# Moving the splits of the second half's weights over slots 54 to 61 in an attention and FFN kernel

## The chip, the cores and the metric

The kernel runs on one core of one Trainium2 chip. The metric is the device time of one launch in microseconds (us); the kernel before took 2179.8 us, the median of three runs (2177.97 to 2180.97). TensorE (PE) does the matrix products, VectorE (DVE), ScalarE (ACT) and GpSimd (POOL) the element-wise work, and SyncE (SP) issues nearly all DMAs (transfers) from one queue, in order.

## The reference

x is 4096 tokens by 512. One layer of linear attention, a layer norm, an FFN with Hadamard transforms, and a second layer norm:

```python
q, k, v = x @ Wq.T, x @ Wk.T, x @ Wv.T      # 16 query heads, 4 key/value heads of 128
q, k = rope(q), rope(k)
qf, kf = elu(q) + 1, elu(k) + 1
# running over the tokens: state += k v^T, z += k; out = (q state) / (q z + eps)
x = layernorm(x + out @ Wo.T)
x = layernorm(x + ffn(x))
```

The change lies in the attention part alone.

## The kernel before

**Precision by splitting.** All products are of float32 accuracy, made of the rounded type float32r: an operand is split into a high half and a low half, and a product is three matmuls (high by high, high by low, low by high). `hilo` does a split: ScalarE copies the raw tile into the high half (line 94), and VectorE or GpSimd subtracts the high half from the raw one to make the low half (line 95).

**Two halves.** The attention runs twice over the tokens: the first half with query heads 0 to 7 and key/value heads 0 and 1, the second with the others. Each half has 16 blocks of 256 tokens. A half's weights are twelve tiles of 128 x 512: eight of q, two of k, two of v. Their high and low halves, 24 tiles, stay in the pool `wres` (28 tiles) for the whole half.

**Slots.** A loop runs over 128 slots, four for each block: slot i works at block n = i // 4, key/value head g and pair of chunks p. In slot i, in the order of the program, the kernel does the query projection of slot i + 5 (`proj_q`, 24 matmuls, line 339), and by the slot's place in its block the key projection of block n + 1 (`proj_k`, first slot, also line 339), the value projection of block n + 1 (`proj_v`, second slot, line 287, tile `ps_v`), the transposes of k (third slot, line 376, `pt`) or the state (line 391, `ps_s`). `ps_v`, `pt` and `ps_s` share one PSUM buffer, so `ps_v` can start when VectorE has read the last `ps_s` (line 402). Then come the scores of slot i + 1 (lines 434 and 435), the product with v and the state, `av` (lines 468 and 469), and last the finishing of the scores of slot i + 1: VectorE lines 444 and 445, GpSimd two `affine_select` (line 448). ScalarE copies `av`'s result out at line 472, its last step in a slot but for a small copy (line 477) in every second one. Rotary work: ScalarE lines 319 and 320, GpSimd line 321, VectorE 322, 325, 329, ScalarE 326 and 420, VectorE 422.

**The change of weights.** The second half starts at slot 64, so its projections are due from slot 59 on: heads q(0,0) and q(0,1) in slot 59, q(0,2), q(0,3) and both tiles of k in slot 60, q(1,0), q(1,1) and both of v in slot 61, q(1,2) and q(1,3) in slot 62. `turn(i)`, called at the end of slot i, reads raw weights (`fetch`) and splits them (`splits`); V or G says which engine makes the low half. Raw tiles are put into `praw` (three buffers, free again when the low half has been made) or into free tiles of `wres`.

**What sets the order.** The Tile framework's planner orders each engine's instructions by modelled times: one that is traced later may be put ahead of one that is not ready. `pin` (and `dma(..., True)`) keeps an instruction behind the one traced just before it on its engine. So a pinned low half on GpSimd in `turn(i)` stands behind the last `affine_select` of slot i + 1's scores, one on VectorE behind line 445 of these, a high half behind ScalarE's last copy of slot i, and a raw read on SP's queue behind the DMAs of slot i. In a slot at the second place of its block the last of these are the four `vd` writes of `proj_v`.

```python
i = S.activation(hi, src, AF.Copy)                              # line 94
j = eng.tensor_tensor(lo, src, hi.bitcast(F32), ALU.subtract)   # line 95
```

Of the kernel before, what the change touches and what calls it, by code (L numbers as in the profile page):

```python
# [43 lines left out]
def kernel(  # L44
# [6 lines left out]
    V, S, G, T = nc.vector, nc.scalar, nc.gpsimd, nc.tensor  # L51

    def dma(dst, src, pin=False):
        if dst.dtype == F32R:
            dst = dst.bitcast(F32)
        if src.dtype == F32R:
            src = src.bitcast(F32)
        i = nc.sync.dma_start(dst, src)  # L58
        if pin:
            tc.keep_in_program_order(i)  # L60

    cpool = ctx.enter_context(tc.tile_pool(name="cpool", bufs=1))
    wres = ctx.enter_context(tc.tile_pool(name="wres", bufs=28))
    praw = ctx.enter_context(tc.tile_pool(name="praw", bufs=3))
# [28 lines left out]
    def hilo(hi, lo, src, eng=V, pinned=False):  # L93
        i = S.activation(hi, src, AF.Copy)  # L94
        j = eng.tensor_tensor(lo, src, hi.bitcast(F32), ALU.subtract)  # L95
        if pinned:
            pin(i)
            pin(j)
# [87 lines left out]
    with ExitStack() as es:  # L186
# [39 lines left out]
        def turn(i):  # L226
            q = lambda g, h: (("q", 1, g, h), wq[8 + 4 * g + h])
            k = lambda g: (("k", 1, g), wk[2 + g])
            v = lambda j: (("v", 1, j), wv[1, :, j * 512:(j + 1) * 512])
            splits = {55: [(q(0, 0), V), (q(0, 1), G)], 56: [(q(0, 2), V)], 57: [(q(0, 3), G), (k(0), V)],  # L230
                      58: [(k(1), V), (q(1, 0), G)], 59: [(q(1, 1), G), (v(0), V), (v(1), V)],
                      60: [(q(1, 2), G), (q(1, 3), V)]}
            fetch = {53: [q(0, 0), q(0, 1), q(0, 2)], 55: [k(0), k(1), q(0, 3)],
                     56: [q(1, 0), q(1, 1), v(0), v(1), q(1, 2), q(1, 3)]}
            for (key, _), eng in splits.get(i, ()):
                hi, lo = (wres.tile([128, 512], F32R, tag="w", name=n) for n in ("wh", "wl"))
                hilo(hi, lo, RAW0.pop(key), eng, True)
                W[key] = hi, lo
            for m, (key, src) in enumerate(fetch.get(i, ())):
                pool, tag = (praw, "raw") if i == 53 or m < (2 if i == 55 else 1) else (wres, "w")  # L240
                RAW0[key] = pool.tile([128, 512], F32, tag=tag, name="raw")
                dma(RAW0[key], src, True)

# [347 lines left out]
        for i, (n, g, p) in enumerate(slots):  # L591
# [61 lines left out]
            for x in gsc:  # L653
                go(x)
            gq = gq2
            turn(i)
            if i == 107:
                o_load(0, None, None)
# [407 lines left out]
    with ExitStack() as es:  # L1066
# [23 lines left out]
        for n in range(NS):  # L1090
# [15 lines left out]
            for s, tag in enumerate(SEQ):  # L1106
# [3 lines left out]
                for u in (1, 0):  # L1110
# [3 lines left out]
                    i = 0  # L1114
# [11 lines left out]
                    if s in (1, 4, 6):  # L1126
                        src, k, q = {1: (ps, 0, 0), 4: (bank.get(("b", u)), 4, 3), 6: (ps, 2, 1)}[s]
# [68 lines left out]
    with ExitStack() as es:  # L1196
# [54 lines left out]
        for idx, (n, s) in enumerate(order):  # L1251
# [25 lines left out]
            tag = SEQ[s]  # L1277
# [14 lines left out]
            i = 0  # L1292
# [98 lines left out]
```

## Time and profile before

| what | value |
|---|---|
| median of the runs | 2179.8 us |
| profiled execution: own time; span | 2179.87 us; 2178.2 us |
| busy, share of the span: PE, DVE, ACT, POOL | 98%, 79%, 63%, 61% |
| granted TensorE clock | 0.997 |
| attention loop on PE (line 339, first and last start) | 8.9 to 827.2 us |
| one block in the second half (four slots) | 25.44 us |

Where the slots lie in time is read from ScalarE's copy at line 472, one for each slot:

| slot | 53 | 54 | 55 | 56 | 57 | 58 | 59 | 60 | 61 | 62 |
|---|---|---|---|---|---|---|---|---|---|---|
| starts at, us | 386.36 | 390.74 | 396.85 | 406.95 | 414.10 | 418.79 | 425.62 | 434.05 | 443.02 | 449.70 |

Times in timelines are counted from the start of the span. "Busy" of PE overstates its work, since one matmul's record of some 0.28 us covers the issue of the next ones, which start every 0.113 us; so the number of matmuls in a stretch is read beside the busy time. What stands in brackets at the end of a line of the timeline is the engine's idle time ahead of the instruction, and what ended it.

### The profile page before, as it was taken

The numbers are of one execution on the slowest core, as the hardware profiler recorded it, in microseconds if no ns is written. First come the engines' busy times: TensorE is split into PE (matmuls) and PEld (weight loads), VectorE is DVE, ScalarE is ACT, GpSimd is POOL, SyncE is SP. The second block draws the span as 40 slices with busy tenths as digits, with TensorE's granted clock in tenths as the row PEclk, the third lists the DMA queues.
The fourth block names the chain that finished last, engine by engine and source line by source line (L and its number), as shares of the span: only waits on it lengthen the run. The fifth ranks groups of instructions, "written<-read, shape, count | busy, mean of one in ns | idle before, by whom it ended". The sixth has DMA issues, their size and how long they took to land.

```text
span 2178.2 us, 42193 instructions
## 1 busy us (share of the span) xinstructions
PE 2140.6 (98%) x14319; PEld 1947.6 (89%) x14319; DVE 1728.9 (79%) x2675; ACT 1378.9 (63%) x2490; POOL 1321.8 (61%) x1104
## 2 busy tenths in 40 slices
PE   8999999999999998999999999999999999999998
PEld 8999999999999997887788788888888888999998
DVE  8999999899999997888998766776866766675655
ACT  8877877777777775443444476655655655565554
POOL 5777767666666666487888256565655555543332
PEclk9999999999999999999999999999999999999999
DMA  6666666656666666989988886876766767897784
GB/s 225 214 221 212 225 220 200 211 183 196 190 201 202 208 187 226 348 245 292 281 289 265 272 277 219 248 243 196 248 207 193 249 191 211 263 307 256 234 261 140
DMA packets 360553, 503.88 MB, mean 231 GB/s; under 512 B 68012, under 2 KB 187052, under 8 KB 356498
## 3 DMA queue, kind: packets, MB, share of 16 engines
q1 hardware_dynamic: 360338, 501.19, 72.1%
q8 instruction: 113, 1.85, 0.4%
q14 instruction: 102, 0.84, 0.1%
HBM read 282.76 MB, written 156.76 MB: 202 GB/s over the span
## 4 chain that ended last, share of the span: by engine, by line
PE 68%; DVE 12%; DMA 7%; issue 4%; POOL 4%; ACT 3%; SPq 2%; DVEq 0%; POOLq 0%; ACTq 0%
PE ps_a L1117 14%; PE ps_qk L339 12%; PE ps_da L1298 8%; PE ps_b L1117 7%; PE ps_wo L180 7%; PE ps_num L468 4%; PE ps_db L1298 4%; PE ps_c L1117 4%; PE ps_v L287 2%; DMA rb<-rec_d 2%; PE ps_dc L1298 2%; SPq L58 2%; DVE ps_qk L322 1%; PE ps_s L391 1%; DMA yraw<-yq_d 1%
## 5 line engine op out<-in xcount | busy, mean ns | idle before, releaser
L339 PE MATMUL ps_qk<-xh,wh 128*128 128x256 f32 x1280 | 354.9, 277 | 1.6 <-DVE x L325 0.9
L339 PE MATMUL ps_qk<-xh,wl 128*128 128x256 f32 x1280 | 354.0, 277 | 0.0
L339 PE MATMUL ps_qk<-xl,wh 128*128 128x256 f32 x1280 | 353.7, 276 | 0.0
L1099 POOL TENSOR_TENSOR cc<-cc 128x512 f32<-128x512 f32 x96 | 146.1, 1525 | 270.4 <-ACT cc L1096 129.5
L95 DVE TENSOR_TENSOR wol<-A,woh 128x512 fp32r<-128x512 f32 x217 | 226.4, 1050 | 94.7 <-ACT woh L94 84.0
L448 POOL TENSOR_SCALAR_AFFINE_SELECT A<-A 64x512 fp32r<-64x512 f32 x256 | 202.7, 792 | 131.1 <-DVE am L444 91.2
L321 POOL TENSOR_TENSOR sw<-sw,csb 128x512 f32<-128x512 f32 x160 | 213.9, 1337 | 76.2 <-ACT sw L320 64.8
L339 PEld LDWEIGHTS ps_qk<-xh,wh 128*128 128x128 f32 x1280 | 240.5, 188 | 4.7 <-DVE ql L422 1.5
L339 PEld LDWEIGHTS ps_qk<-xh,wl 128*128 128x128 f32 x1280 | 240.5, 188 | 1.5 <-DVE wl L95 0.2
L339 PEld LDWEIGHTS ps_qk<-xl,wh 128*128 128x128 f32 x1280 | 240.4, 188 | 1.0
L94 ACT ACTIVATE woh<-A 128x512 fp32r<-128x512 f32 x217 | 135.0, 628 | 122.5 <-PE ps_b L1117 72.8
L1117 PE MATMUL ps_a<-yoh,woh 128*128 128x512 f32 x512 | 199.9, 391 | 3.1 <-ACT sv L1124 2.6
L95 POOL TENSOR_TENSOR hal<-hraw,hah 128x512 fp32r<-128x512 f32 x74 | 98.1, 1327 | 172.7 <-PE ps_da L1298 59.6
L1117 PE MATMUL ps_a<-yol,woh 128*128 128x512 f32 x512 | 199.4, 389 | 0.0
L94 ACT ACTIVATE hah<-hraw 128x512 fp32r<-128x512 f32 x212 | 132.1, 631 | 106.3 <-PE ps_da L1298 54.2
L1117 PE MATMUL ps_a<-yoh,wol 128*128 128x512 f32 x512 | 196.7, 390 | 0.0
L95 DVE TENSOR_TENSOR hal<-hraw,hah 128x512 fp32r<-128x512 f32 x138 | 99.2, 727 | 90.1 <-PE ps_da L1298 39.0
L1124 ACT ACTIVATE sv<-ps_a,wsc 128x512 f32<-128x512 f32 x192 | 126.8, 679 | 34.7 <-PE ps_a L1117 34.4
L180 PE MATMUL ps_wo<-wh,oh 128*128 128x512 f32 x368 | 144.4, 393 | 0.0
L180 PE MATMUL ps_wo<-wh,ol 128*128 128x512 f32 x368 | 144.0, 391 | 0.0
L180 PE MATMUL ps_wo<-wl,oh 128*128 128x512 f32 x368 | 143.5, 390 | 0.0
L868 POOL TENSOR_TENSOR o<-nt,rb 128x512 f32<-128x512 f32 x62 | 86.8, 1400 | 74.0 <-DVE ol L95 44.1
(306 smaller groups left out, 7274.4 us busy)
## 6 DMA issues: line engine op xcount, KB each, us to landing
hraw<-hop_d SPq DMA_DIRECT2D x224, 256.0 KB
num_d<-num SPq DMA_DIRECT2D x128, 256.0 KB
rb<-rec_d SPq DMA_DIRECT2D x128, 256.0 KB
hop_d<-hS SPq DMA_DIRECT2D x128, 256.0 KB
vd<-vhl SPq DMA_DIRECT2D x128, 252.0 KB
nt<-num_d SPq DMA_DIRECT2D x30, 1024.0 KB
A<-in_wug_dram SPq DMA_DIRECT2D x93, 256.0 KB
hop_d<-cc SPq DMA_DIRECT2D x64, 256.0 KB
```

The source lines that it names most:

```text
L94: i = S.activation(hi, src, AF.Copy)
L95: j = eng.tensor_tensor(lo, src, hi.bitcast(F32), ALU.subtract)
L180: T.matmul(ps, l[:, h], r, start=i == 0, stop=i == 47)
L321: G.tensor_tensor(sw, sw, sinb, ALU.mult)
L339: T.matmul(ps[:, j], W[key][wa][:, k * 128:(k + 1) * 128], B[xa][:, k], start=i == 0, stop=i == 11)
L448: G.affine_select(ah, ah.bitcast(F32), pattern=[[0, 8], [1, 64]], compare_op=ALU.is_ge, fill=0.0, base=0, channel_multiplier=-1)
L468: T.matmul(ps[:, c2], l, r, start=i == 0, stop=i == len(ops) - 1)
L868: i = G.tensor_tensor(o32, c["nt"][:, 4 * g:4 * g + 4], rb, ALU.mult)
L1099: G.tensor_tensor(x, x, c.pop(("g", q)), ALU.mult)
L1117: T.matmul(ps, w[:, u, k], y[:, k], start=first and i == 0, stop=i == 5, skip_group_check=not first)
L1124: S.activation(x, ps, AF.Copy, scale=sc)
L1298: T.matmul(pj[j], ops[qd][al][:, r, js], BW[s][bl][ip], start=first and (i == 0 or i == 3 and pj is ps), stop=i >= 45 or last and i == 23, ...
```

## The change

Which slot splits which tile, and on which engine the low half is made; one `turn` per slot:

| slot | before: splits | after: splits | before: reads | after: reads |
|---|---|---|---|---|
| 52 | | | | q00, q01, q02 |
| 53 | | | q00, q01, q02 | |
| 54 | | q00 V | | q03 |
| 55 | q00 V, q01 G | q01 G | k0, k1, q03 | k0 |
| 56 | q02 V | q02 V, q03 G | q10, q11, v0, v1, q12, q13 | k1, v0, v1 |
| 57 | q03 G, k0 V | k0 V | | q10 |
| 58 | k1 V, q10 G | k1 V, v0 G | | q11, q12 |
| 59 | q11 G, v0 V, v1 V | q10 V, v1 G | | q13 |
| 60 | q12 G, q13 V | q11 G | | |
| 61 | | q12 G, q13 V | | |

VectorE makes six low halves in place of seven, GpSimd six in place of five. The number of reads and of high halves stays at twelve each. One raw tile (v1) is put into `wres` in place of six.

```diff
-            splits = {55: [(q(0, 0), V), (q(0, 1), G)], 56: [(q(0, 2), V)], 57: [(q(0, 3), G), (k(0), V)],
-                      58: [(k(1), V), (q(1, 0), G)], 59: [(q(1, 1), G), (v(0), V), (v(1), V)],
-                      60: [(q(1, 2), G), (q(1, 3), V)]}
-            fetch = {53: [q(0, 0), q(0, 1), q(0, 2)], 55: [k(0), k(1), q(0, 3)],
-                     56: [q(1, 0), q(1, 1), v(0), v(1), q(1, 2), q(1, 3)]}
+            splits = {54: [(q(0, 0), V)], 55: [(q(0, 1), G)], 56: [(q(0, 2), V), (q(0, 3), G)], 57: [(k(0), V)],
+                      58: [(k(1), V), (v(0), G)], 59: [(q(1, 0), V), (v(1), G)], 60: [(q(1, 1), G)],
+                      61: [(q(1, 2), G), (q(1, 3), V)]}
+            fetch = {52: [q(0, 0), q(0, 1), q(0, 2)], 54: [q(0, 3)], 55: [k(0)], 56: [k(1), v(0), v(1)],
+                     57: [q(1, 0)], 58: [q(1, 1), q(1, 2)], 59: [q(1, 3)]}
...
-                pool, tag = (praw, "raw") if i == 53 or m < (2 if i == 55 else 1) else (wres, "w")
+                pool, tag = (wres, "w") if (i, m) == (56, 2) else (praw, "raw")
```

## The prediction

> **What bounds the kernel now.** I first read the page: PE is busy 98% of the span, at a granted clock of 0.997, so only time in which PE stands still can be won. Then I cut the attention into stretches of one block (25.44 us). These are the lines of four of them; the columns are the stretch, its length, each engine's busy time with its number of instructions, the granted clock, and DMA's share and rate.
>
> ```profile
> 378.70:404.20 25.50, 25.40 (x222) 24.92 (x221) 21.43 (x35) 19.27 (x36) 13.33 (x15) 1.00 0.56 169
> 404.20:429.60 25.40, 23.96 (x199) 22.85 (x199) 23.90 (x41) 21.75 (x42) 18.69 (x18) 1.00 0.79 252
> 429.60:455.00 25.40, 22.35 (x184) 21.18 (x184) 24.58 (x38) 18.41 (x35) 15.62 (x16) 1.00 0.34 109
> 480.50:505.90 25.40, 25.40 (x226) 25.17 (x226) 23.93 (x39) 20.07 (x38) 16.98 (x17) 1.00 0.61 194
> ```
>
> The two middle stretches, where the weights change, hold 199 and 184 matmuls against 226 in a full one: 27 and 42 missing, at 0.113 us each 3.1 + 4.7 = 7.8 us. That is all that this change can win where it stands. The fourth line shows PE full again afterwards, so a loss or gain here reaches the end of the attention whole.
>
> Next I asked who waited for whom between 390 and 455 us (sum, times, longest).
>
> ```profile
> PE ps_v L287 <- DVE s L402: 3.4, 2, 2.5
> ...
> ACT wh L94 <- DMA raw<-in_wq_dram: 3.0, 1, 3.0
> ...
> DVE wl L95 <- ACT wh L94: 2.6, 1, 2.6
> ```
>
> PE waits for VectorE (the buffer that `ps_v` takes over), ScalarE once for a raw weight, VectorE for ScalarE behind it. The timelines of ACT, SP, PE, DVE and POOL place these waits.
>
> ```profile
> 400.68 0.64 ACT L94 ACTIVATE wh<-raw 128x512 fp32r<-128x512 f32 x1 [2.99 <-DMA raw<-in_wq_dram]
> ...
> 390.27 3.88 SPq L58 DMA_DIRECT2D vd<-vhl  x4
> 394.21 2.57 SPq L58 DMA_DIRECT2D raw<-in_wq_dram  x3
> ...
> 418.90 4.20 SPq L58 DMA_DIRECT2D vd<-vhl  x4
> 423.20 0.72 SPq L58 DMA_DIRECT2D xh<-xs_d  x1
> ...
> 406.44 0.38 PE L287 MATMUL ps_v<-wh,xh 128*128 128x256 f32 x1 [0.89 <-DVE s L402]
> 436.71 0.35 PE L287 MATMUL ps_v<-wh,xh 128*128 128x256 f32 x1 [2.48 <-DVE s L402]
> ...
> 431.56 2.38 DVE L95 TENSOR_TENSOR wl<-raw,wh 128x512 fp32r<-128x512 f32 x2
> 436.16 0.41 DVE L402 TENSOR_TENSOR s<-ps_s,s 128x256 f32<-128x256 f32 x1
> ...
> 431.05 1.74 POOL L321 TENSOR_TENSOR sw<-sw,csb 128x512 f32<-128x512 f32 x1
> 440.56 1.29 POOL L95 TENSOR_TENSOR wl<-raw,wh 128x512 fp32r<-128x512 f32 x1
> ```
>
> The read of q00 in slot 53 is issued at 394.21, behind four `vd` writes, and lands 6.44 us later; ScalarE, ready since 397.69, stands 2.99 us. VectorE, busy almost without a break from 375 to 448 us, loses 2.64 us by that. It comes late to line 402 twice, and PE waits 0.89 and 2.48 us. Before the second wait stand both v splits (2.31 us up to the next instruction's start). q12's low half is made at 440.56 to 441.85, and PE takes it up at 441.91, after `av` of slot 61 was put between: no time to spare with two slots' distance.
>
> **The change part by part.** The sum is made against the profiled execution, 2179.87 us (span 2178.2 and 1.67 around it), 0.07 above the median.
>
> Reads of slot 53 go to slot 52. They then stand on SP behind `num` of slot 52 (381.36, 0.34 long) and ahead of the `vst` and `vd` writes. SP is idle from 381.7 to 386.32, and three issues at 0.33 to 0.43 us, or 2.57 as now, fit. DMA's share is 0.03 at 380 to 382 us and 0.36 in the next two, so they land by about 388; ScalarE wants q00 in slot 54 at 391.3 (390.74 + 0.58). The 2.99 us wait goes, and with it PE's 0.89: **-0.9** (ends -1.7 if the stall's tail, 0.42 at 420.50 and 0.4 at 451, went too, and 0 if VectorE stays late for its splits).
>
> The read of q10 goes from slot 56 to 57, behind the `vd` writes of that slot. These are issued to 423.1; the `xh` read next in line, issued at 423.20, is complete by the trace's semaphore updates at 428.97. ScalarE wants q10 behind slot 59's copies, at 426.4. So the same wait as in slot 55 comes back, 428.97 - 426.4 = 2.6 us. Queued behind it on ScalarE are v1's high half, two rotary copies and the exponent of slot 60, and the scores' copy (line 441); VectorE, PE and GpSimd wait for these. By the first stall's price this is +0.9; it takes back VectorE's lag that the first part won, which I have not counted. I take 0 beyond that, ends 0 and +2.6.
>
> Of v's two low halves and q11's, the split work ahead of the wait at 436.71 becomes one on VectorE (q10, 0.69 undisturbed) in place of two (2.31): **-1.6**, ends -2.5 (the whole wait) and 0 (if ScalarE's late copies hold VectorE up). v1's low half on GpSimd in slot 59 ends where q11's does now, 431.1, or 2.6 later with the read's delay: 433.7, still ahead of `ps_v`'s place.
>
> One more split on GpSimd takes 1.29 of POOL's time; POOL was busy 13.3 to 18.7 us of 25.4, so that is hidden. But VectorE's instructions with two SBUF inputs are slow beside it: the splits pair above started under POOL's 1.74 us `sw` and took 1.1 us over two undisturbed ones; **+0.3** as a quarter of that, ends 0 and +1.1. The Trainium skill, "SBUF — State Buffer", section "Who interferes with whom", says that VectorE's two-input instruction and a GpSimd instruction reading SBUF lock each other out for a whole instruction. That speaks against moving splits to GpSimd: by the rule the extra split can cost VectorE its whole 1.29 once, which would make this sum +1.4 us; by the row it costs a part of that, and the sum goes by the row.
>
> q11 now has one slot's distance in place of two, q12 and q13 one in place of two. Their places on GpSimd are behind the second `affine_select` of slots 61's and 62's scores. From the undisturbed rows: the scores at 459.43 have their last `affine_select` over at 465.18 (5.8 us), those at 466.68 at 473.00 (6.3); with 1.29 for the split, a low half is there 7.1 and 7.6 us after the scores' matmuls start. For q11, PE has in that time scores 0.45, `av` 1.25, q10's 12 matmuls 1.36 and two of q11's 0.23: 3.3, so 3.8 us are open. `ps_v` (24 x 0.113 = 2.7) and `av` of slot 61 (1.25, free before the split is made) fill them if the planner puts them ahead: **0**, ends 0 and +9.2 (VectorE as late as now: 429.31 to 440.48, + 1.29, - 3.3). For q12, PE has scores 0.45, `av` 1.25, q11's 1.36, transposes 0.44, two matmuls 0.23 and `av` of slot 62 1.25: 5.0 of 7.6, so **+2.6**; ends 0 (slot 63's projection, 2.7, goes first, as it does at 445.57 now, ahead of `av` of slot 62) and +7.8 (439.96 to 448.20, + 1.29, less the first, second and fifth term, 1.7, with nothing put between). q13's low half on VectorE ends earlier than q12's.
>
> The raw reads into `praw` make SP wait for low halves: in slot 58 for v0's on GpSimd (about 425 us), in slot 59 for q10's (about 432). Behind these stand `num` writes (three buffers) and block 17's x, wanted at 445. The next `vst` writes come at 445.04. This costs **0**, ends 0 and +1 (one late `xh`, as priced by PE's wait of 0.89).
>
> Sum: -0.9 - 1.6 + 0.3 + 2.6 = +0.4; 2179.87 + 0.4 = 2180.3, or **2180.2** against the median.
>
> **The rivals.** *Even* (the forecast): what VectorE gains is spent by the one-slot distance. For it speaks that PE's order at 440.54 already goes around a late q12. Own range 2175.5 to 2184.2, 0.2% (4.4 us, about what a measurement tells from none) on each side.
>
> *Slower*: one mechanism, PE standing at q11 and q12 with nothing put between. It costs 3.8 + 5.9 (7.6 - 1.7) - 2.5 won + 0.3 = +7.5, 2187.4; with VectorE as late as now 9.2 + 7.8 - 2.5 + 0.3 = +14.8, 2194.7. It decides once PE's waits there pass 6.6 us (4.4 + 2.5 - 0.3). For it: the planner's modelled times do not see waits such as those of 2.99 and 2.48 us, or it would have filled them. Against: it filled at 440.79.
>
> *Faster*: VectorE is on time, PE's gaps close, and slot 63's projection covers q12. Six of the 7.8 us come back: 2173.9. Against: q10's read.
>
> *The stall only moves*, from slot 55 to 59, and nothing else changes: -0.9 + 0.9, within the even case.
>
> **How the numbers follow.** Even 0.43, slower 0.37, faster 0.20. The range leaves out half of the faster case (below 2174.5) and the upper part of the slower (above 2190.5), about 0.1 each: 2174.5 to 2190.5.
>
> **What would show it.** ScalarE's wait for a raw weight gone near 398 and back near 426, ended by q10; `ps_v`'s second wait under 1.5 us; GpSimd's low half of q12 right before PE's next projection, with a wait of 2 to 3 us there; 200 to 215 matmuls in both stretches. I am wrong if the planner orders slots 59 to 63 otherwise than now, if stretches after 455 us change, or if PE waits over 5 us at q11 or q12.

## The result and the profile after

The changed kernel takes 2200.03 us (median of six runs, 2193.48 to 2201.81) against 2180.26 for the kernel before in the same comparison (six runs). The medians lie 19.8 us apart, a ratio of 1.0091. The ratio on record, which is not the quotient of the medians here or below, is 1.0068, 95% interval 1.0048 to 1.0089: 10 to 19 us slower. The prediction was 2180.2, range 2174.5 to 2190.5.

Two executions of one kernel can differ by some 11 us in the last stage (in some, of any of these kernels, its matmuls follow each other every 0.117 us and not every 0.112, at a granted clock of 1.00), so the experiments below are also compared by the start of the attention's last projection matmul, which lies ahead of that stage. It is the second number of the range in these lines, from the view of the tile `ps_qk` (operation and tiles, count, shortest/median/longest in ns, first and last start, forms). Before:

```profile
L339 PE MATMUL ps_qk<-xh,wl x1280: 275/276/388, 11.4 to 827.3; 128*128 128x256 f32 x183
```

After:

```profile
L339 PE MATMUL ps_qk<-xh,wl x1280: 276/276/415, 11.1 to 846.9; 128*128 128x256 f32 x183
```

The attention ends 19.6 us later. So nearly all that was lost was lost there. By stretches of one block in the changed kernel (the stretch, its length, busy time and number of instructions of PE, PEld, DVE, ACT and POOL, the granted clock, DMA's share and rate):

```profile
353.30:378.80 25.50, 25.50 (x227) 25.26 (x227) 23.68 (x38) 19.66 (x37) 15.41 (x16) 1.00 0.50 161
378.80:404.20 25.40, 20.03 (x145) 16.98 (x144) 19.45 (x34) 16.09 (x31) 13.62 (x15) 0.97 0.56 178
404.20:429.60 25.40, 21.94 (x180) 21.31 (x181) 15.20 (x26) 15.68 (x29) 15.16 (x15) 0.96 0.62 197
429.60:455.10 25.50, 17.67 (x131) 16.87 (x130) 18.49 (x30) 14.53 (x26) 9.85 (x10) 0.87 0.51 149
```

The full first stretch shows that nothing is lost before 378 us. Then 82, 47 and 96 matmuls are missing against 227 (before it was 5, 28 and 43). VectorE, which had hardly a break in these blocks before (21.43 to 24.58 us busy of some 25.4), is now idle for a good part of them (15.20 us busy of 25.40): it no longer sets the pace. Who waited for whom between 380 and 460 us:

```profile
DVE am L444 <- ACT A L441: 13.7, 3, 6.6
...
ACT xh L94 <- DMA raw<-in_x_t_dram: 9.6, 2, 5.4
...
PE ps_qk L339 <- ACT qh L420: 5.9, 1, 5.9
...
ACT wh L94 <- DMA raw<-in_wq_dram: 5.4, 1, 5.4
PE ps_qk L339 <- ACT xh L94: 5.4, 2, 2.9
```

ScalarE's wait for a raw q weight in slot 55, which I had followed, and both of PE's ahead of `ps_v` are gone (the wait for `in_wq` above is a later one). In its place ScalarE waits 9.6 us for raw **x**, a load that the change does not name. The view of the tile `raw` says when x was split (first and last start in the window), and SP's timeline when it was read. Before:

```profile
L94 ACT ACTIVATE xh<-raw x2: 617/624/632, 364.1 to 364.6; 128x512 fp32r<-128x512 f32 x2
...
L58 SPq DMA_DIRECT2D raw<-in_x_t_dram x1: 425/425/425, 350.8 to 350.8; - x1
...
323.61 0.94 SPq L58 DMA_DIRECT2D raw<-in_x_t_dram  x2
```

After:

```profile
L58 SPq DMA_DIRECT2D raw<-in_x_t_dram x2: 367/484/602, 397.4 to 404.2; - x2
L94 ACT ACTIVATE xh<-raw x2: 629/629/629, 401.8 to 410.5; 128x512 fp32r<-128x512 f32 x2
```

This is block 15's x, the last block that the first half reads raw. Its two reads are traced in slot 53 and use two of the three `praw` buffers. Before, they ran far ahead of their place in the program: one was issued in the pair at 323.61 us (the other of that pair is block 14's second), one at 350.82, and both were split at 364 to 368. The reads of q00, q01, q02, in slot 53's `turn`, came behind them. Moved to slot 52 they are traced ahead of x, and take all three buffers; x gets one back only when q00's low half is made, and the second only after q01's. The timelines of the changed kernel show this row by row (SP, DVE, POOL, ACT, PE).

```profile
378.88 1.69 SPq L58 DMA_DIRECT2D raw<-in_wq_dram  x3
...
392.44 0.95 DVE L95 TENSOR_TENSOR wl<-raw,wh 128x512 fp32r<-128x512 f32 x1
...
397.56 1.28 POOL L95 TENSOR_TENSOR wl<-raw,wh 128x512 fp32r<-128x512 f32 x1
...
397.40 0.60 SPq L58 DMA_DIRECT2D raw<-in_x_t_dram  x1
...
404.25 0.37 SPq L58 DMA_DIRECT2D raw<-in_x_t_dram  x1
...
401.83 0.63 ACT L94 ACTIVATE xh<-raw 128x512 fp32r<-128x512 f32 x1 [5.43 <-DMA raw<-in_x_t_dram]
...
410.46 0.63 ACT L94 ACTIVATE xh<-raw 128x512 fp32r<-128x512 f32 x1 [4.18 <-DMA raw<-in_x_t_dram]
...
402.51 0.81 PE L339 MATMUL ps_qk<-xh,wh 128*128 128x256 f32 x3 [2.50 <-ACT xh L94]
...
411.15 0.62 PE L339 MATMUL ps_qk<-xh,wh 128*128 128x256 f32 x3 [2.87 <-ACT xh L94]
```

q00's buffer is free at 393.4 and the first x read follows at 397.4; q01's is free at 398.8 and the second follows at 404.25. So 4.0 and 5.4 us of the delay pass on SP's queue, where other transfers now stand ahead of x, in the second case one that waits for the first half of x itself (`xs_d<-xh` at 402.83). PE, which wants block 15's x from slot 55 on, is short of work for most of the time from 388 to 412 us. Later the read of q10, behind `vd` as foreseen, brings a second stall, twice as long as foreseen:

```profile
426.78 4.04 SPq L58 DMA_DIRECT2D vd<-vhl  x4
430.86 3.41 SPq L58 DMA_DIRECT2D raw<-in_wq_dram  x3
...
437.76 0.63 ACT L94 ACTIVATE wh<-raw 128x512 fp32r<-128x512 f32 x1 [5.44 <-DMA raw<-in_wq_dram]
...
442.80 0.55 PE L339 MATMUL ps_qk<-xh,wh 128*128 128x256 f32 x1 [5.91 <-ACT qh L420]
```

### The profile page after: what moved, and what is told of

Its sections match the earlier page's. It is cut to its first block, busy times and chain, and to the rows that moved or that the text cites. A ratio compares the mean times of both kernels' runs of the same rounds, so it can differ in the third digit from the quotient of the medians.

```text
span 2199.9 us, 42192 instructions
## 1 busy us (share of the span) xinstructions
PE 2147.1 (98%) x14319; PEld 1951.3 (89%) x14319; DVE 1729.7 (79%) x2674; ACT 1378.8 (63%) x2490; POOL 1319.1 (60%) x1105
## 4 chain that ended last, share of the span: by engine, by line
PE 71%; DVE 13%; DMA 6%; issue 3%; ACT 3%; POOL 3%; SPq 1%; DVEq 0%; POOLq 0%; ACTq 0%
PE ps_a L1117 14%; PE ps_wo L180 11%; PE ps_qk L339 11%; PE ps_da L1298 7%; PE ps_b L1117 7%; PE ps_db L1298 4%; PE ps_num L468 4%; PE ps_c L1117 3%; PE ps_v L287 2%; PE ps_dc L1298 2%; DVE ps_qk L322 2%; SPq L58 1%; PE ps_s L391 1%; DVE A L445 1%; DVE am L444 1%
## 5 line engine op out<-in xcount | busy, mean ns | idle before, releaser
L339 PE MATMUL ps_qk<-xh,wh 128*128 128x256 f32 x1280 | 356.0, 279 | 14.7 <-ACT qh L420 5.9
L322 DVE TENSOR_TENSOR ps_qk<-ps_qk,csb 128x512 f32<-128x512 f32 x160 | 111.1, 695 | 28.5 <-ACT sw L320 23.6
```

The source lines that it names most:

```text
L322: V.tensor_tensor(ps, ps, cosb, ALU.mult)
L339: T.matmul(ps[:, j], W[key][wa][:, k * 128:(k + 1) * 128], B[xa][:, k], start=i == 0, stop=i == 11)
```

## The experiments

The theory after the result, **X**: the three raw buffers, taken ahead of block 15's x, hold it back. Beside it **Q**: the read of q10 lands too late. The rival, **L**, is the prediction's own slower case: q11, q12 and q13 are split one slot ahead of their use. Times stand in a table at the end of this section.

**Reads alone (b52).** The kernel before, with the first three reads in slot 52.

```diff
-            fetch = {53: [q(0, 0), q(0, 1), q(0, 2)], 55: [k(0), k(1), q(0, 3)],
+            fetch = {52: [q(0, 0), q(0, 1), q(0, 2)], 55: [k(0), k(1), q(0, 3)],
...
-                pool, tag = (praw, "raw") if i == 53 or m < (2 if i == 55 else 1) else (wres, "w")
+                pool, tag = (praw, "raw") if i == 52 or m < (2 if i == 55 else 1) else (wres, "w")
```

> The kernel before, with the read of q00, q01, q02 alone moved from slot 53 to 52; the splits stay. Theory X: the three raw buffers are then taken ahead of block 15's raw x (traced in slot 53), which is read only when the first q splits have freed them; in the changed kernel that made ScalarE wait 5.4 and 4.2 us for raw x. Here the first split is a slot later still, so PE waits longer: 10 to 22 us slower than before, 2190 to 2202. Theory L (the rival of the prediction: q11, q12 and q13 split only one slot ahead of their use): nothing is late here, and ScalarE's wait of 2.99 us goes: 0 to 3 us faster, 2177 to 2180.

2204.02 us, ratio 1.010 (1.0065 to 1.0136); the attention ends at 843.9, 16.6 us later than before. That is a little above the 2190 to 2202 that I expected. One slot, 53 to 52 (the second place keeps the three reads in the three raw buffers), makes nearly the whole loss, 16.6 of 19.6 us, with every split where it was. The waits for x in it, from 376 to 462 us:

```profile
ACT xh L94 <- DMA raw<-in_x_t_dram: 6.1, 2, 5.9
...
PE ps_qk L339 <- ACT xh L94: 4.9, 1, 4.9
```

**Block 15's x ahead of the reads (ax).** The changed kernel, with `load_x(15)` called in slot 52, so traced before `turn(52)`.

```diff
             if sl == (0, 0):
...
+                if n + 2 == NB - 1:
+                    run(load_x(n + 2))
             elif sl == (0, 1):
...
-                if n + 2 < N:
+                if n + 2 < N and n + 2 != NB - 1:
                     run(load_x(n + 2))
```

> The changed kernel, with block 15's x read and split one slot earlier in the program (slot 52, ahead of the reads of q). Theory X: the two waits for raw x go, and with them 9.6 us on PE (13.4 us lost from 382 to 412 us, against 3.8 before), 2188 to 2192; PE's wait of 5.9 us behind the read of q10 stays. Theory L: the time stays within 3 us of 2200.

2179.56 us, ratio to before 0.9993 (0.9965 to 1.002). The attention ends at 822.8: 24.1 us won back, where I expected some 10 (2188 to 2192): with x in time the wait for q10 shrinks too, from 5.4 to 1.6 us on ScalarE, and PE has none from it. First the view of `raw`, then the waits from 376 to 462 us:

```profile
L94 ACT ACTIVATE xh<-raw x2: 617/624/632, 362.9 to 363.5; 128x512 fp32r<-128x512 f32 x2
```

```profile
ACT wh L94 <- DMA raw<-in_wq_dram: 1.6, 1, 1.6
...
PE ps_v L287 <- DVE s L402: 1.4, 1, 1.4
```

**The same with q10 read one slot earlier (axq, axq5).**

```diff
-            fetch = {52: [q(0, 0), q(0, 1), q(0, 2)], 54: [q(0, 3)], 55: [k(0)], 56: [k(1), v(0), v(1)],
-                     57: [q(1, 0)], 58: [q(1, 1), q(1, 2)], 59: [q(1, 3)]}
+            fetch = {52: [q(0, 0), q(0, 1), q(0, 2)], 54: [q(0, 3)], 55: [k(0)], 56: [k(1), v(0), v(1), q(1, 0)],
+                     58: [q(1, 1), q(1, 2)], 59: [q(1, 3)]}
...
-                pool, tag = (wres, "w") if (i, m) == (56, 2) else (praw, "raw")
+                pool, tag = (wres, "w") if i == 56 and m > 1 else (praw, "raw")
```

> As ax, and q10's raw read moved from slot 57 to 56, into the larger pool, ahead of the four vd writes. Theory X with Q (the read of q10 behind these writes lands too late): ScalarE's 5.4 us wait at 438 goes too and PE's 5.9 us with it, 2180 to 2184. Theory L: 2190 or more, since q11 to q13 are still split one slot ahead.

2176.38 us (expected 2180 to 2184), ratio 0.9972 (0.9949 to 0.9995), attention's end 822.6. Against ax that is 0.2 us: without X, the late read costs PE next to nothing. Theory L, which wanted 2190 or more here, falls. It was run again:

> Both reads mended once more, with more rounds, to settle whether it beats the kernel before: 3 to 6 us faster (the attention's last projection ended at 822.6 us against 827.3 in the kernel before, 4.7 us). If what was measured the first time was chance: within 1.5 us.

2180.66 us against 2183.48, ratio 0.9982 (0.9962 to 1.0003). The gain was seen again, smaller, and this interval reaches just past one; the attention ended at 825.0 in this profile, 2.3 us earlier than before.

**The splits late alone (blate).** The kernel before with q11 in slot 60 and q12, q13 in slot 61.

```diff
-                      58: [(k(1), V), (q(1, 0), G)], 59: [(q(1, 1), G), (v(0), V), (v(1), V)],
-                      60: [(q(1, 2), G), (q(1, 3), V)]}
+                      58: [(k(1), V), (q(1, 0), G)], 59: [(v(0), V), (v(1), V)],
+                      60: [(q(1, 1), G)], 61: [(q(1, 2), G), (q(1, 3), V)]}
```

> The kernel before, with q11 split in slot 60 and q12, q13 in slot 61, so one slot ahead of their use as in the changed kernel; nothing else moves. Theory L: 7.5 to 14.8 us slower as the prediction's slower case had it, 2187 to 2195. Theories X and Q: the raw reads are where they were, so 0 to 3 us slower, 2180 to 2183.

2185.72 us against 2182.18, ratio 1.0015 (0.9991 to 1.0039), attention's end 829.5, 2.2 us later. The median lies between what the two theories expected, and the interval, up to 8.5 us, would still admit the low end of L's 7.5 to 14.8; the attention's end does not. PE has no wait for a split in this window; its waits are of the kind it had before, for VectorE ahead of `ps_v`, somewhat longer (4.5 us against 3.4):

```profile
PE ps_v L287 <- DVE s L402: 4.5, 2, 3.1
PE ps_s L391 <- DVE ps_qk L325: 1.0, 1, 1.0
```

**q10's read alone (aq).** The changed kernel with the edit of axq, and x left where the change put it.

> The changed kernel with q10's raw read alone moved from slot 57 to 56, into the larger pool; block 15's x stays where the change put it. Theory Q: PE's wait of 5.9 us at 442.8 goes, the loss from 382 to 412 us stays: 5 to 8 us faster than the changed kernel, 2192 to 2195. If that wait is only a result of block 15's lateness, the time stays at 2198 to 2201.

2199.29 us, ratio to before 1.0077 (1.0045 to 1.0109); attention's end 842.0, 4.9 us earlier than in the changed kernel. That is just short of the 5 to 8 that Q named. The times do not show it: 0.7 us between medians of different sets of runs, and 2199.29 lies where the other theory wanted it (2198 to 2201). In the trace PE's 5.9 us wait for `qh` is gone, and the 9.3 us wait for raw x stays. So by one profile of each kernel Q is a stall of its own, some 4 to 5 us, but only where x is already late.

**Buffers or queue (axb).** In ax, x was also moved ahead on SP's queue. Here it stays in slot 53, behind the reads of q, and only gets buffers of the larger pool.

```diff
                     raw = RAW0.pop(("x", n, j), None)
+                    if n == NB - 1:
+                        raw = wres.tile([128, 512], F32, tag="w", name="raw")
+                        dma(raw, x_t[b, :, c])
```

> The changed kernel with block 15's two raw x tiles in the larger pool; it stays traced in slot 53, behind the reads of q in slot 52. If the three raw buffers are what held block 15's x back, its waits go and the attention's last projection ends within 3 us of the 822.8 us of the kernel that traced it earlier (changed kernel: 846.9); 2176 to 2182. If the place on SP's queue behind the reads of q is the cause, the attention still ends after 840 us and the time stays at 2192 or more.

2179.11 us against 2183.48, ratio 0.9977 (0.9956 to 0.9998); attention's end 822.7, within 0.1 of ax. The three buffers are the cause: with others, the planner runs both reads ahead to 349 us, though they are traced behind those of q. The place on SP's queue, where a part of the delay passed, changes with them.

```profile
L58 SPq DMA_DIRECT2D raw<-in_x_t_dram x2: 333/832/1330, 349.1 to 349.5; - x2
```

**What the parts are worth.** The kernel before with early reads, and x ahead of them (b52x, both edits shown above); with v's low halves on GpSimd (bvg); and, as a control, with x traced in slot 52 alone (bx).

```diff
-                      58: [(k(1), V), (q(1, 0), G)], 59: [(q(1, 1), G), (v(0), V), (v(1), V)],
+                      58: [(k(1), V), (q(1, 0), G)], 59: [(q(1, 1), G), (v(0), G), (v(1), G)],
```

> The kernel before, with the first reads in slot 52 and block 15's x read and split ahead of them; the splits stay as before. By theory X this has what the earlier reads were worth by themselves: ScalarE's 2.99 us wait at 397.7 gone, PE's 0.9 us and some of VectorE's lateness: 1 to 4 us faster than before. If spreading the splits is what made the kernel with both late reads mended 5.8 us faster, this one stays within 1.5 us of before.

> The kernel before with v's two low halves on GpSimd in slot 59, nothing else. The prediction's term: VectorE is spared 2.31 us ahead of the read that PE waits for, so PE's 2.48 us wait shrinks to under 1 us: 1 to 2.5 us faster. Rival: GpSimd makes three splits in slot 59 (3.9 us), v's low halves come 2.6 us later, PE waits for these: 0 to 2 us slower.

> A control: the kernel before with block 15's x traced in slot 52 and not 53, nothing else. In the trace of before it was already read at 350.8 and split at 364 to 368 us, ahead of its place in the program, so nothing should move: within 1 us of before. If moving this load is a gain by itself, what the mended kernels won is partly not theirs.

By the times all three are within noise: 2187.95, 2179.43 and 2187.79 us against 2184.25, ratios 1.0005 (0.9983 to 1.0026), 0.9988 (0.9968 to 1.0007) and 1.0004 (0.9976 to 1.0031). By the attention's end the control stands at 827.4 (+0.1), the early reads at 823.8 (-3.5) and v on GpSimd at 826.6 (-0.7). In bvg PE's second wait is indeed short, but in the way of the rival PE now waits for GpSimd too, for splits and for an `affine_select` ahead of `av`:

```profile
PE ps_num L468 <- POOL A L448: 1.0, 1, 1.0
PE ps_v L287 <- DVE s L402: 0.8, 1, 0.8
PE ps_v L287 <- POOL wl L95: 0.5, 2, 0.4
```

**All mended, splits two slots ahead (best).** On the changed kernel with x in slot 52:

```diff
-            splits = {54: [(q(0, 0), V)], 55: [(q(0, 1), G)], 56: [(q(0, 2), V), (q(0, 3), G)], 57: [(k(0), V)],
-                      58: [(k(1), V), (v(0), G)], 59: [(q(1, 0), V), (v(1), G)], 60: [(q(1, 1), G)],
-                      61: [(q(1, 2), G), (q(1, 3), V)]}
+            splits = {54: [(q(0, 0), V)], 55: [(q(0, 1), G)], 56: [(q(0, 2), V), (q(0, 3), G)], 57: [(k(0), V), (q(1, 0), G)],
+                      58: [(k(1), V), (v(0), G)], 59: [(q(1, 1), V), (v(1), G)], 60: [(q(1, 2), V), (q(1, 3), G)]}
-            fetch = {52: [q(0, 0), q(0, 1), q(0, 2)], 54: [q(0, 3)], 55: [k(0)], 56: [k(1), v(0), v(1)],
-                     57: [q(1, 0)], 58: [q(1, 1), q(1, 2)], 59: [q(1, 3)]}
+            fetch = {52: [q(0, 0), q(0, 1), q(0, 2)], 54: [q(0, 3)], 55: [k(0), q(1, 0)], 56: [k(1), v(0), v(1), q(1, 1)],
+                     58: [q(1, 2), q(1, 3)]}
...
-                pool, tag = (wres, "w") if (i, m) == (56, 2) else (praw, "raw")
+                pool, tag = (wres, "w") if (i == 56 and m > 1) or (i, m) == (55, 1) else (praw, "raw")
```

> Block 15's x traced in slot 52, and all of q(1,*) split two slots or more ahead of use: q10 on GpSimd in slot 57, q11 on VectorE in 59, q12 on VectorE and q13 on GpSimd in 60; q10 and q11 read into the larger pool. If the one-slot distance of q11, q12 and q13 still costs something, the attention ends 1 to 2 us before that of the kernel with both reads mended (822.6 us); if the planner fills it, within 0.7 us of it.

2181.25 us against 2183.48, ratio 0.9968 (0.9949 to 0.9988): of all intervals here the one that lies furthest below one, though the medians are only 2.2 us apart. Its attention ends at 822.5, 0.1 us from axq, so two slots' distance in place of one is worth nothing that can be told here.

| kernel | edit | ratio to before (95%) | attention's end, us | against before | counted from block 12, against before |
|---|---|---|---|---|---|
| before | | | 827.3 | | |
| after | the change | 1.0068 (1.0048 to 1.0089) | 846.9 | +19.6 | +18.9 |
| b52 | reads alone | 1.0100 (1.0065 to 1.0136) | 843.9 | +16.6 | +17.2 |
| ax | after, x first | 0.9993 (0.9965 to 1.0020) | 822.8 | -4.5 | -3.4 |
| axb | after, x in other buffers | 0.9977 (0.9956 to 0.9998) | 822.7 | -4.6 | -4.1 |
| axq | ax, q10 read earlier | 0.9972 (0.9949 to 0.9995) | 822.6 | -4.7 | -4.3 |
| axq5 | axq again | 0.9982 (0.9962 to 1.0003) | 825.0 | -2.3 | -4.2 |
| aq | after, q10 read earlier | 1.0077 (1.0045 to 1.0109) | 842.0 | +14.7 | +15.1 |
| blate | late splits alone | 1.0015 (0.9991 to 1.0039) | 829.5 | +2.2 | +2.7 |
| b52x | reads alone, x first | 1.0005 (0.9983 to 1.0026) | 823.8 | -3.5 | -2.6 |
| bvg | v on GpSimd alone | 0.9988 (0.9968 to 1.0007) | 826.6 | -0.7 | +0.1 |
| bx | x first alone | 1.0004 (0.9976 to 1.0031) | 827.4 | +0.1 | +0.5 |
| best | axq's idea, two slots ahead | 0.9968 (0.9949 to 0.9988) | 822.5 | -4.8 | -4.4 |

The attention's end is from one profile each; axq and axq5, the same kernel, differ by 2.4 us, of which 2.2 were there before the change of weights (value projection of block 12 at 327.3 and 329.5 us). So differences below some 2 us in the last column but one are not told apart from chance. The last column counts the attention's end from the first matmul of that value projection (`ps_v`: 327.67 us before, 328.33 after, 329.54 in axq5, 326.60 to 327.33 in the others). There axq and axq5 agree within 0.1 us and the control stands at +0.5, so it tells more; what differs by less than 1 us in it is still not told apart.

## Why the prediction was wrong

- **"Reads of slot 53 go to slot 52"** is the step that failed. I costed the move at -0.9 (ends -1.7 and 0), and looked at SP's queue, the landing time and ScalarE's need, but not at the buffers that the three reads take and who else was to have them (for the later reads into `praw` I did ask that). By b52 the term is +16.6 us at the attention's end, +17.2 counted from block 12. The trace of before held the sign: the `raw` view shows x of block 15 split at 364 us, twenty us ahead of its slot 53 (386.36), so it lived on running ahead; and the program has only three such buffers. The -3.5 of b52x (-2.6 counted from block 12) is what the step is worth when x has its buffers: more than the 0.9 that I gave it. That VectorE then comes less late to all that follows is a likely reason, not one that a run isolates.
- **q10's read behind `vd`** was foreseen in place and cause. Its size was not: 5.44 us on ScalarE in place of 2.6, 5.91 on PE, and 4.9 us at the attention's end (aq; 3.8 counted from block 12), where I took 0 with an end of +2.6. Alone it is harmless (ax to axq, 0.2 us; 0.9 counted from block 12). The price was right for a kernel that is on time and wrong for one that is already late.
- **One slot's distance for q11, q12, q13**, +2.6 with ends up to +9.2 and +7.8: blate gives +2.2 alone (+2.7 counted from block 12), near the forecast, best against axq 0.1. My reason for a small number, that the planner puts other work on PE in the open time, fits blate, where PE has no wait for a split; my fear in the slower rival does not. That rival was on the right side of the result, with 2187.4 to 2194.7, by a mechanism that the runs exclude as its cause.
- **v's low halves on GpSimd**, -1.6 + 0.3: bvg gives -0.7 at the attention's end and +0.1 counted from block 12, so no gain is shown. PE's second wait does shrink, from 2.48 to 0.8 us, but PE then waits 1.5 us for GpSimd, whose extra work I had taken as hidden.
- **The sum without the failed step.** Everything but the buffers gives -4.5 (ax; -3.4 counted from block 12) where I had +0.4. The ceiling of 7.8 us, read from missing matmuls, is not passed by any kernel here. But that a gain in these two blocks reaches the end whole was wrong: axq wins back 25 and 30 of the missing matmuls, 6.2 us, and ends 4.7 us earlier (4.3 counted from block 12), for it has 3 and 14 matmuls fewer than before in the two blocks that follow.

```profile
404.20:429.60 25.40, 25.40 (x224) 25.11 (x222) 24.99 (x41) 21.67 (x40) 18.25 (x18) 1.00 0.79 258
429.60:455.00 25.40, 24.77 (x214) 24.06 (x213) 22.14 (x38) 20.55 (x39) 17.86 (x18) 1.00 0.53 166
455.00:480.50 25.50, 25.50 (x224) 25.24 (x223) 24.83 (x38) 20.01 (x38) 16.85 (x17) 1.00 0.59 190
480.50:505.90 25.40, 24.62 (x212) 23.87 (x211) 24.29 (x39) 19.32 (x37) 17.14 (x18) 1.00 0.53 171
```

- Of the signs that I named for being wrong, PE waiting over 5 us at q11 or q12 is not what came; the 5.91 us wait stands in the same place but ends with ScalarE's `qh`, queued behind q10. That stretches after 455 us change did come, as the last line above shows; why that block loses them is not tested.

## What to carry to other kernels

Before a load is moved, list the buffers that it takes and every other tile that shares them, and look in the trace whether one of these runs ahead of its place in the program: such a load pays nothing where it is written, and all of it when a new claim is traced before it. A price for a stall that is read from a kernel on time need not hold in one that is late: here the late read of q10 cost 0.2 us alone and 4.9 behind the first stall. Mend the buffer conflict first, and only then judge the change: here it was a gain of 3 to 5 us in the attention under a loss of 24.

## What the hardware showed unexpectedly

PE's granted clock fell to half in the wake of two stalls of the changed kernel. Columns: stretch, length, busy of PE, PEld, DVE, ACT, POOL, granted clock, DMA.

```profile
402.00:403.00 1.00, 0.49 (x3) 0.49 (x4) 0.03 (x1) 1.00 (x3) 0.46 (x1) 0.89 0.79 256
403.00:406.00 3.00, 2.76 (x13) 2.47 (x13) 1.35 (x2) 1.24 (x3) 2.93 (x4) 0.50 0.79 195
...
440.00:441.00 1.00, 0.00 (x0) 0.00 (x0) 0.84 (x2) 0.98 (x3) 0.80 (x1) 0.66 0.87 195
441.00:444.00 3.00, 1.20 (x5) 1.23 (x6) 2.94 (x5) 2.69 (x6) 1.62 (x3) 0.50 0.56 202
444.00:447.00 3.00, 3.00 (x16) 3.00 (x16) 2.97 (x6) 0.97 (x2) 2.92 (x3) 0.50 0.35 87
```

The clock record has it at half for 3.4 us from 402.8 and for 6.8 us from 440.3. The 24 matmuls from 442.80 to 447.66 took 4.9 us where 24 x 0.113 = 2.7 is usual, so the second one added about 2.1 us to the stall that caused it. The kernel before, whose longest wait here was 2.48 us, kept its full clock in the same blocks. The Trainium skill, "TensorE: Matmul & The Clock Gate", Part 1, says that PE drops to half speed after at least one idle window of about 3.4 us. The second stall (PE idle from 436.9 to 442.8) agrees; the first does not quite, since the longest unbroken wait ahead of 402.8 was 2.50 us, though PE had been sparsely used since 388. Nor is the longest wait alone what decides: one of 2.87 us, up to 411.15, cost no clock. In the 3.42 us ahead of the first fall (399.36 to 402.78) PE was busy for 0.85 us; in the next but one and the one after it (406.19 to 409.60 and 409.60 to 413.02), which share the 2.87 us wait, for 2.08 and 1.87. The two falls stand 11 times 3.41 us apart, so that low use within a fixed step of that length brings the fall would fit these rows; no run here tests it.
